# An expert step moved to the last group of attention heads and cut into column-tiled pieces

## Chip, cores and metric

One of the cores of a Trainium2 chip runs the kernel. The metric is the device time of one execution in microseconds (us); lower is better. TensorE (PE) multiplies matrices, VectorE (DVE) and GpSimd (POOL) work elementwise and reduce, ScalarE (ACT) applies functions, SyncE (SP) issues transfers. GpSimd issues transfers too; those of GpSimd share one queue, q0.

## What is computed

The input x has 4 sequences of 2048 tokens of 512 numbers. The output is x, plus attention with 16 heads of 32, plus a layer in which every token goes to one of 8 experts, each of which takes its first 100 tokens:

```python
def reference(x, w_qkv, w_out, b_out, mask_logits, w_gate, w_expert, b_expert):
    xn = layernorm(x)
    # attention
    q, k, v = split(xn @ w_qkv)                  # 16 heads of 32
    q, k = spectral_filter(q), spectral_filter(k)
    attn = softmax(q @ k.T / sqrt(32))
    a = (attn @ v) @ w_out + b_out
    # experts
    probs = softmax(xn @ w_gate)                 # 8 experts
    best, gate = argmax(probs), max(probs)
    place = cumsum(one_hot(best)) - 1            # place in the expert's list
    kept = place < 100                           # the first 100 of each expert
    e = gate * kept * (xn @ w_expert + b_expert) # the other tokens get nothing
    return x + a + e
```

All experts have the same weights w_expert, so the layer is one product of at most 800 gathered rows with a 512 x 512 matrix.

## The kernel before

The heads are taken in 16 groups k of four (4 sequences x 4 groups, `NG = 4`). A group has four blocks n of 512 queries, a block has 16 tiles of 128 keys, and the work on one key tile is called a half (`HB = 16` halves a block, `GH = 64` a group); two halves, an even and an odd one, are a window. Groups, blocks and halves are counted from 0; "half 37 of group 15" lies in its block 2.

In each half TensorE makes the scores of four heads (`scores`, 32-row tiles), ScalarE takes their exponentials from PSUM into an even or an odd tile of 1 MB (two ACTIVATEs of 128x1024), and TensorE multiplies the tile of the half before with the values (`products`, 32-column tiles), which VectorE adds to `num`. Beside that TensorE makes scores of a later block once more, only for the row maxima (`max_matmuls`), and VectorE reduces them (`max_reduce`, `part<-array`); they run 42 places, that is 21 halves, ahead, so the last 21 halves of the last group have none. The maxima enter the scores as a product with ones (`shift`, `array<-negm,ones_b`) at the start of each block.

For the sums over keys, a transfer of GpSimd adds the odd tile into the even one (`pair`, `even<-odd`, an accumulating DMA, issued a window later), and GpSimd adds the even tiles of successive windows (`add_to`, two windows later; without maxima VectorE does it, three windows later). There are three odd and five even tiles. In the next block, `close_steps` folds the last tile into row sums on TensorE (half 5), inverts them on VectorE (halves 6 to 13, 64 columns each), multiplies on GpSimd (`divide`, `ot`, half 14), projects with w_out (four pieces at halves 17 to 20, that is, 1 to 4 of the block after) and adds the result y to the output with an accumulating DMA of 1 MB (`out_dram<-y`, half 21). For block 2 of the last group these places are 7, 8 to 11, 12, 12 to 15 and 15. The last block is closed by `close_last` after the loop, into a copy of the output rows that SyncE has loaded before (`y`, named xs there).

Everything is issued in program order on each compute engine (`InOrder`). The extra steps are hung into an agenda by half with `at(half, step, cost=...)`, where a cost of 1 is a projection piece (16 matmuls of 128 rows x 32 columns x 128 outputs, `columns`, lines 417 to 421). `plan(k)` makes the projections of group k + 1 in group k; `spread` (line 899) places its 48 pieces evenly over the halves, given the costs that are already there. Group 15 has no next group and no projections. Where the cost of a half is not zero, the maxima of the second pair of heads may be reduced in one instruction instead of two (line 1095).

The experts (`expert_steps`, lines 568 to 642, placed by `place_experts`, lines 939 to 955) run so, with `start` = half 0 of group 12:

- half 36 of group 12: `begin` loads w_exp and b_exp, reads the four tables of (token, gate) entries that the routing of the last sequence has filled, merges them and clears `xg`, 7 tiles of 128 rows;
- halves 38 to 50: `fetch` gathers the rows of x by indirect DMA; halves 42 to 54: `measure`; half 58: `scale`;
- half 62 of group 12 to half 14 of group 13, every second half: `expert(i)` normalizes a tile on ScalarE, turns the tile before it (four transposes on TensorE, copied to `xt`, one buffer), and multiplies the one before that (four matmuls of 128 x 128 x 512), adds the bias on VectorE and weighs with the gate on ScalarE;
- from half 26 of group 13, a row tile a block: `gather_row` reads the output rows by indirect DMA on GpSimd (half 26 of the block), `add_row` adds on GpSimd two halves later, `scatter_row` writes them back by indirect DMA two halves after that. The seventh is scattered at the start of group 15.

Gather and scatter read and write the whole output as far as dependences are concerned, so each waits for accumulations of y issued before it, and an accumulation after it waits for the scatter.

Of the kernel before, what the change touches and what calls it, by code (L numbers as in the profile page):

```python
# [12 lines left out]
F32 = mybir.dt.float32  # L13
BF16 = mybir.dt.bfloat16
I32 = mybir.dt.int32
AF = mybir.ActivationFunctionType
ALU = mybir.AluOpType
# [8 lines left out]
P = 128  # L26
# [4 lines left out]
QB = 512  # L31
# [70 lines left out]
def attention_and_top1_experts(ctx: ExitStack, tc: tile.TileContext, a: dict, out: bass.AP):  # L102
# [14 lines left out]
    def bank():  # L117

        return array[:, next(turns), :]
# [445 lines left out]

    taken = {}

    def expert_steps():


        def begin():
            w_exp = chunk("w_exp")
            on.sync.dma_start(out=w_exp, in_=a["L0_ffn_w_expert"].rearrange("(r p) n -> p r n", p=P))
            b_exp = work.tile([P, DM], F32, tag="b_exp", name="b_exp", bufs=1)
            on.sync.dma_start(out=b_exp, in_=a["L0_ffn_b_expert"].partition_broadcast(P))
            entries = small.tile([P, NTAB, ST, 2], F32, name="entries")
            for i, table in enumerate(tables):
                on.sync.dma_start(out=entries[:, i], in_=table.rearrange("(t p) c -> p t c", p=P))
            entry = small.tile([P, ST, 2], F32, name="entry1")
            for i, op in enumerate((ALU.min, ALU.max)):  # L580
                on.vector.tensor_reduce(
                    entry[:, :, i], entries[:, :, :, i].rearrange("p n t -> p t n"), AX.X, op
                )
            who = small.tile([P, ST], I32, name="who")
            on.vector.tensor_copy(who, entry[:, :, 0])
            xg = [chunk("xg"), small.tile([P, ST - TQ, DM], F32, name="xg1")]
            for half in xg:
                on.gpsimd.memset(half, 0.0)
            mv = small.tile([P, ST, 2], F32, name="mv1")
            index = [bass.IndirectOffsetOnAxis(ap=who[:, i : i + 1], axis=0) for i in range(ST)]  # L590
            bound = {"bounds_check": B * S - 1, "oob_is_err": False}
            taken.update(mv=mv, w_exp=w_exp, b_exp=b_exp, entry=entry, index=index, bound=bound, xg=xg)

        def row(i):
            return taken["xg"][i // TQ][:, i % TQ, :]
# [15 lines left out]
            on.gpsimd.tensor_scalar(shift, shift, -1.0, None, ALU.mult)  # L611
            taken.update(rstd=rstd, shift=shift)

        def expert(i):

            if i >= 2:
                at = slice(i - 2, i - 1)
                pe = bank()
                for r in range(NR):
                    on.tensor.matmul(  # L620
                        pe,
                        lhsT=taken["xt"][:, r * P : (r + 1) * P],
                        rhs=taken["w_exp"][:, r, :],
                        start=(r == 0),
                        stop=(r == NR - 1),
                    )
                on.vector.tensor_tensor(row(i - 2), pe, taken["b_exp"], ALU.add)
            if 1 <= i <= ST:
                px = bank()
                for r in range(NR):  # L630
                    on.tensor.transpose(px[:, r * P : (r + 1) * P], row(i - 1)[:, r * P : (r + 1) * P], ident)
                taken["xt"] = work.tile([P, QB], F32, tag="byx", name="xt", bufs=1)
                on.scalar.copy(taken["xt"], px)
            if i >= 2:
                on.scalar.activation(row(i - 2), row(i - 2), AF.Copy, scale=taken["entry"][:, at, 1])
            if i < ST:
                at = slice(i, i + 1)
                on.scalar.activation(
                    row(i), row(i), AF.Identity, bias=taken["shift"][:, at], scale=taken["rstd"][:, at]
                )  # L640

        return begin, fetch, measure, scale, expert

    def gather_row(i):
        taken["sum"] = work.tile([P, DM], F32, tag="byx", name="yg", bufs=1)
        on.gpsimd.indirect_dma_start(taken["sum"], None, out_rows, taken["index"][i], **taken["bound"])

    def add_row(i):
        row = taken["xg"][i // TQ][:, i % TQ, :]
        on.gpsimd.tensor_tensor(row, row, taken["sum"], ALU.add)  # L650

    def scatter_row(i):
        row = taken["xg"][i // TQ][:, i % TQ, :]
# [285 lines left out]
    def place_experts(start):  # L939


        begin, fetch, measure, scale, expert = expert_steps()
        first = start + 36
        at(first, begin)
        for i in range(ST):
            at(first + 2 + 2 * i, fetch, i)
            at(first + 6 + 2 * i, measure, i)
        at(first + 22, scale)
        for i in range(ST + 2):
            at(first + 26 + 2 * i, expert, i, cost=(NR if i >= 2 else 0) + (1 if 1 <= i <= ST else 0))  # L950
        for i in range(ST):
            free = start + GH + i * HB + 26
            for step in (gather_row, add_row, scatter_row):
                at(free, step, i)
                free += 2

    def plan(k):

# [87 lines left out]
    for block in range(1, B * NG * NQ):  # L1046

        costs[block * HB - 5] += 0.25
    place_experts((B - 1) * NG * GH)
    for k in range(B * NG):  # L1050
        plan(k)

# [107 lines left out]
```

## Time and profile before

| | us |
|---|---|
| median of 3 runs | 4195.3 (4194.85 to 4196.63) |
| the profiled execution | 4199.95 |
| its span, first to last instruction | 4197.9 |
| TensorE busy | 4154.1 |
| VectorE busy | 3436.8 |
| GpSimd busy | 2968.2 |
| ScalarE busy | 2493.4 |

In the groups of instructions, the columns are line, engine, operation, written and read tiles, shapes, count, then busy time, mean ns of one, and the idle time before them with what ended it. All have line 82 (the helper that pins the order), so one goes by the tiles' names.

```profile
L82 DVE TENSOR_REDUCE part<-array 128x1 f32<-128x512 f32 (+1 forms) x3129 | 2484.2, 849 | 671.1 <-PE array L82 662.4
L82 POOL TENSOR_TENSOR even<-even 128x1024 f32<-128x1024 f32 x876 | 2121.7, 2524 | 434.6 <-DMA even<-odd 433.6
L82 PE MATMUL array<-keys,q 32*128 32x512 f32 x8192 | 2061.1, 613 | 15.8 <-DVE part L82 5.8
L82 PE MATMUL array<-q,steps_of_keys 32*128 32x512 f32 x8192 | 2029.3, 615 | 2.4 <-ACT odd L82 2.3
L82 ACT ACTIVATE odd<-array 128x1024 f32<-128x1024 f32 x1024 | 995.7, 1021 | 489.4 <-PE array L82 412.7
L82 PE MATMUL array<-xnT,w 128*32 128x128 f32 x16384 | 527.4, 273 | 1.4 <-DVE part L82 0.6
```

An f32 matmul stands in the trace as two records, so 8 records of w_exp are 4 matmuls and 32 of a projection piece are 16. The queue of GpSimd carries most of the traffic; the columns are packets, MB and the share of 16 DMA engines' time:

```profile
q0 software_dynamic: 110432, 605.83, 73.8%
q1 hardware_dynamic: 67952, 71.34, 5.3%
```

### The profile page before, as it was taken

How to read it: one execution, taken by the hardware profiler on the slowest of the kernel's cores; microseconds unless marked ns; L12 is line 12 of the kernel's file. 1: busy time of each engine (PE TensorE's matmuls, PEld its weight loads, DVE VectorE, ACT ScalarE, POOL GpSimd, SP SyncE). 2: the span in 40 equal slices, each digit the busy share in tenths (PEclk: the TensorE clock that was granted, in tenths of full speed). 3: DMA queues.
4: the chain of work that ended last, by engine and by line, in shares of the span. 5: the costliest groups of instructions: out<-in, count | busy, mean ns of one | idle time of the engine just before them, and what ended most of it. 6: DMA issues, size and time to landing. Idle time of an engine off the chain costs nothing.

```text
span 4197.9 us, 121495 instructions
## 1 busy us (share of the span) xinstructions
PE 4154.1 (99%) x52846; PEld 1852.0 (44%) x52846; DVE 3436.8 (82%) x4952; ACT 2493.4 (59%) x3436; POOL 2968.2 (71%) x2052
## 2 busy tenths in 40 slices
PE   8999999999999999999999999999999999999998
PEld 5444444444444444444444444444444443444432
DVE  7778888977888888897788888888778888788896
ACT  4555566675655556657565556666656555556665
POOL 1578676776876777776687766767668776677873
PEclk9999999999999999999999999999999999999999
DMA  3677878987787788898678778799877986778788
GB/s 120 141 149 154 163 152 168 222 194 144 144 166 157 152 160 161 194 202 183 137 155 163 155 156 159 156 200 202 173 151 142 183 162 132 152 159 167 154 168 176
DMA packets 178990, 684.97 MB, mean 163 GB/s; under 512 B 23494, under 2 KB 53352, under 8 KB 113176
## 3 DMA queue, kind: packets, MB, share of 16 engines
q0 software_dynamic: 110432, 605.83, 73.8%
q1 hardware_dynamic: 67952, 71.34, 5.3%
q8 instruction: 414, 6.78, 0.6%
q14 instruction: 120, 0.98, 0.1%
q10 hardware_dynamic: 72, 0.03, 0.0%
HBM read 71.07 MB, written 87.91 MB: 38 GB/s over the span
## 4 chain that ended last, share of the span: by engine, by line
PE 93%; DVE 4%; DMA 1%; issue 1%; ACT 1%; POOL 0%; SPq 0%; ACTq 0%; POOLq 0%; DVEq 0%
PE array L82 93%; DVE part L82 3%; DMA even<-odd 1%; DVE num L82 1%; DVE factor L82 0%; ACT odd L82 0%; POOL even L82 0%; DMA odd<-in_L_attn_w_qkv_dram 0%; DMA w<-in_L_attn_w_qkv_dram 0%; ACT even L82 0%; POOL ot L82 0%; DVE even L82 0%; ACT keys L82 0%; ACT xs L82 0%; SPq L82 0%
## 5 line engine op out<-in xcount | busy, mean ns | idle before, releaser
L82 DVE TENSOR_REDUCE part<-array 128x1 f32<-128x512 f32 (+1 forms) x3129 | 2484.2, 849 | 671.1 <-PE array L82 662.4
L82 POOL TENSOR_TENSOR even<-even 128x1024 f32<-128x1024 f32 x876 | 2121.7, 2524 | 434.6 <-DMA even<-odd 433.6
L82 PE MATMUL array<-keys,q 32*128 32x512 f32 x8192 | 2061.1, 613 | 15.8 <-DVE part L82 5.8
L82 PE MATMUL array<-q,steps_of_keys 32*128 32x512 f32 x8192 | 2029.3, 615 | 2.4 <-ACT odd L82 2.3
L82 ACT ACTIVATE odd<-array 128x1024 f32<-128x1024 f32 x1024 | 995.7, 1021 | 489.4 <-PE array L82 412.7
L82 ACT ACTIVATE even<-array 128x1024 f32<-128x1024 f32 x1024 | 994.4, 1021 | 446.2 <-PE array L82 427.4
L82 PEld LDWEIGHTS array<-keys,q 32*128 32x128 f32 x8192 | 772.1, 184 | 583.5 <-DVE part L82 350.1
L82 PEld LDWEIGHTS array<-q,steps_of_keys 32*128 32x128 f32 x8192 | 691.6, 183 | 259.4 <-issue 228.6
L82 POOL DMA_DIRECT2D even<-odd x510 | 469.7, 922 | 377.7 <-ACT odd L82 318.1
L82 DVE TENSOR_TENSOR num<-num,array 128x512 f32<-128x512 f32 x960 | 650.8, 678 | 17.8 <-PE array L82 17.6
L82 PEld LDWEIGHTS array<-xnT,w 128*32 128x32 f32 x16384 | 458.4, 110 | 257.5 <-DVE part L82 175.9
L82 PE MATMUL array<-even,v 128*32 128x512 f32 x4096 | 545.5, 605 | 0.8 <-DVE part L82 0.8
L82 PE MATMUL array<-odd,v 128*32 128x512 f32 x4096 | 545.9, 605 | 0.0
L82 PE MATMUL array<-xnT,w 128*32 128x128 f32 x16384 | 527.4, 273 | 1.4 <-DVE part L82 0.6
L82 PEld LDWEIGHTS array<-w,xnT 128*32 128x32 f32 x8192 | 229.8, 110 | 148.1 <-DVE part L82 102.8
L82 DVE RECIPROCAL factor<-den 128x64 f32<-128x64 f32 x504 | 274.7, 546 | 0.0
L82 PE MATMUL array<-wo,ot 128*32 128x512 f32 x2048 | 266.9, 594 | 5.0 <-POOL ot L82 5.0
L82 PE MATMUL array<-w,xnT 128*32 128x128 f32 x8192 | 269.7, 273 | 1.8 <-DMA w<-in_L_attn_w_qkv_dram 1.6
L82 PEld LDWEIGHTS array<-even,v 128*32 128x32 f32 x4096 | 80.5, 108 | 389.7 <-DVE part L82 378.6
L82 PEld LDWEIGHTS array<-odd,v 128*32 128x32 f32 x4096 | 80.8, 108 | 388.5 <-DVE part L82 378.4
L82 POOL DMA_DIRECT2D out_dram<-y x63 | 85.9, 1364 | 197.4 <-ACT y L82 125.8
L82 ACT COPY q<-array 128x128 f32<-128x128 f32 x256 | 67.9, 265 | 181.1 <-PE array L82 177.3
(129 smaller groups left out, 1484.5 us busy)
## 6 DMA issues: line engine op xcount, KB each, us to landing
even<-odd POOLq DMA_DIRECT2D x510, 1024.0 KB
out_dram<-y POOLq DMA_DIRECT2D x63, 1024.0 KB
xs<-in_L_attn_x_dram SPq DMA_DIRECT2D x96, 256.0 KB
out_dram<-in_L_attn_x_dram SPq DMA_DIRECT2D x16, 1024.0 KB
w<-wd SPq DMA_DIRECT2D x30, 256.0 KB
w<-in_L_attn_w_qkv_dram SPq DMA_DIRECT2D x16, 256.0 KB
wo<-in_L_attn_w_out_dram SPq DMA_DIRECT2D x16, 256.0 KB
negm<-row SPq DMA_DIRECT2D x192, 4.0 KB
```

What stands on the lines that cost most here:

```text
L82: done = act(*args, **kwargs)
```

## The change

The expert step is placed against group 15, the last one (`place_experts` is called with its first half). `begin` is divided: loads and table reads at half 18 of group 14, merging the tables and clearing xg (`sort`) at half 26, then fetches at halves 28 to 40, measurements at 41 to 53 and `scale` at 58. In group 15 the steps of a row tile i take five of the halves that are not 1 to 5 of a block: `normal` two halves ahead, `turn` (cost 0.5), then four `multiply` (cost 1), each for 128 of the 512 outputs with `columns`, with its own bias add of 128x128 on VectorE, and `weigh`. Turns stand at halves 0, 10, 15, 25, 30, 40 and 45, the pieces between them, the last at half 54. `xt` lies alternately in the weight buffers w0 and w1, which no projection uses any more, and gathered output rows in w2 (w1 for the last) and the old buffer. Rows 0 and 1 are gathered at half 24, added at 27 and scattered at 28; rows 2 and 3 at 40, 43, 44; rows 4, 5 and 6 at 56, 59, 60. The last copy of output rows (y) is loaded after those scatters in program order. The work of the layer is the same.

```diff
+    def spent_weights(s):
+        return weights.tile([P, NR, P], F32, name=f"w{s}", bufs=1).rearrange("p r n -> p (r n)")
+
+    def spare_row():
+        return work.tile([P, DM], F32, tag="byx", name="yg", bufs=1)
...
-        def expert(i):
-
-            if i >= 2:
-                at = slice(i - 2, i - 1)
-                pe = bank()
-                for r in range(NR):
-                    on.tensor.matmul(
-                        pe,
-                        lhsT=taken["xt"][:, r * P : (r + 1) * P],
-                        rhs=taken["w_exp"][:, r, :],
-                        start=(r == 0),
-                        stop=(r == NR - 1),
-                    )
-                on.vector.tensor_tensor(row(i - 2), pe, taken["b_exp"], ALU.add)
...
+        def normal(i):
+            at = slice(i, i + 1)
+            on.scalar.activation(
+                row(i), row(i), AF.Identity, bias=taken["shift"][:, at], scale=taken["rstd"][:, at]
+            )
+
+        def turn(i):
+            px = bank()
+            for r in range(NR):
+                on.tensor.transpose(px[:, r * P : (r + 1) * P], row(i)[:, r * P : (r + 1) * P], ident)
+            taken["xt"] = spent_weights(i % 2)
+            on.scalar.copy(taken["xt"], px)
+
+        def multiply(i, quarter):
+            cols = slice(quarter * P, (quarter + 1) * P)
+            pe = bank()[:, cols]
+            for r in range(NR):
+                columns(
+                    pe,
+                    taken["xt"][:, r * P : (r + 1) * P],
+                    taken["w_exp"][:, r, cols],
+                    start=(r == 0),
+                    stop=(r == NR - 1),
                 )
+            on.vector.tensor_tensor(row(i)[:, cols], pe, taken["b_exp"][:, cols], ALU.add)
+
+        def weigh(i):
+            on.scalar.activation(row(i), row(i), AF.Copy, scale=taken["entry"][:, i : i + 1, 1])
...
     def gather_row(i):
-        taken["sum"] = work.tile([P, DM], F32, tag="byx", name="yg", bufs=1)
-        on.gpsimd.indirect_dma_start(taken["sum"], None, out_rows, taken["index"][i], **taken["bound"])
+        taken["sum", i] = spare_row() if i % 2 else spent_weights(2 if i < ST - 1 else 1)
+        on.gpsimd.indirect_dma_start(taken["sum", i], None, out_rows, taken["index"][i], **taken["bound"])
...
-        first = start + 36
-        at(first, begin)
+        at(start - 46, begin)
+        at(start - 38, sort)
         for i in range(ST):
-            at(first + 2 + 2 * i, fetch, i)
-            at(first + 6 + 2 * i, measure, i)
-        at(first + 22, scale)
-        for i in range(ST + 2):
-            at(first + 26 + 2 * i, expert, i, cost=(NR if i >= 2 else 0) + (1 if 1 <= i <= ST else 0))
+            at(start - 36 + 2 * i, fetch, i)
+            at(start - 23 + 2 * i, measure, i)
+        at(start - 6, scale)
+        halves = iter([start + h for h in range(GH) if not 1 <= h % HB <= TQ + 1])
         for i in range(ST):
-            free = start + GH + i * HB + 26
-            for step in (gather_row, add_row, scatter_row):
-                at(free, step, i)
-                free += 2
+            half = next(halves)
+            at(half - 2, normal, i)
+            at(half, turn, i, cost=0.5)
+            for quarter in range(NR):
+                half = next(halves)
+                at(half, multiply, i, quarter, cost=1)
+            at(half + 1, weigh, i)
+        for block, tiles in ((1, (0, 1)), (2, (2, 3)), (3, (4, 5, 6))):
+            for step, half in ((gather_row, 8), (add_row, 11), (scatter_row, 12)):
+                for i in tiles:
+                    at(start + block * HB + half, step, i)
...
-    place_experts((B - 1) * NG * GH)
+    place_experts((B * NG - 1) * GH)
```

More of the change, by code (lines that the diff above doesn't have):

```diff
@@ L578, in begin, with sort @@
                 on.sync.dma_start(out=entries[:, i], in_=table.rearrange("(t p) c -> p t c", p=P))
+            taken.update(w_exp=w_exp, b_exp=b_exp, entries=entries)
+        def sort():
+            entries = taken["entries"]
             entry = small.tile([P, ST, 2], F32, name="entry1")
@@ L591, in begin @@
             bound = {"bounds_check": B * S - 1, "oob_is_err": False}
-            taken.update(mv=mv, w_exp=w_exp, b_exp=b_exp, entry=entry, index=index, bound=bound, xg=xg)
+            taken.update(mv=mv, entry=entry, index=index, bound=bound, xg=xg)
         def row(i):
@@ L612, in scale @@
             taken.update(rstd=rstd, shift=shift)
-        def expert(i):
-            if i >= 2:
-                at = slice(i - 2, i - 1)
-                pe = bank()
-                for r in range(NR):
-                    on.tensor.matmul(
-                        pe,
-                        lhsT=taken["xt"][:, r * P : (r + 1) * P],
-                        rhs=taken["w_exp"][:, r, :],
-                        start=(r == 0),
-                        stop=(r == NR - 1),
-                    )
-                on.vector.tensor_tensor(row(i - 2), pe, taken["b_exp"], ALU.add)
[L628 to L639, printed above, removed]
-                )
@@ L642, in expert_steps @@
-        return begin, fetch, measure, scale, expert
+        def normal(i):
[9 more added lines that the diff above has]
+            on.scalar.copy(taken["xt"], px)
@@ L644, in gather_row @@
+        def weigh(i):
+            on.scalar.activation(row(i), row(i), AF.Copy, scale=taken["entry"][:, i : i + 1, 1])
+        return begin, sort, fetch, measure, scale, normal, turn, multiply, weigh
     def gather_row(i):
-        taken["sum"] = work.tile([P, DM], F32, tag="byx", name="yg", bufs=1)
-        on.gpsimd.indirect_dma_start(taken["sum"], None, out_rows, taken["index"][i], **taken["bound"])
+        taken["sum", i] = spare_row() if i % 2 else spent_weights(2 if i < ST - 1 else 1)
@@ L648, in add_row @@
+        on.gpsimd.indirect_dma_start(taken["sum", i], None, out_rows, taken["index"][i], **taken["bound"])
     def add_row(i):
         row = taken["xg"][i // TQ][:, i % TQ, :]
-        on.gpsimd.tensor_tensor(row, row, taken["sum"], ALU.add)
+        on.gpsimd.tensor_tensor(row, row, taken["sum", i], ALU.add)
     def scatter_row(i):
@@ L939, in place_experts @@
     def place_experts(start):
-        begin, fetch, measure, scale, expert = expert_steps()
-        first = start + 36
-        at(first, begin)
+        begin, sort, fetch, measure, scale, normal, turn, multiply, weigh = expert_steps()
+        at(start - 46, begin)
+        at(start - 38, sort)
         for i in range(ST):
-            at(first + 2 + 2 * i, fetch, i)
-            at(first + 6 + 2 * i, measure, i)
-        at(first + 22, scale)
-        for i in range(ST + 2):
-            at(first + 26 + 2 * i, expert, i, cost=(NR if i >= 2 else 0) + (1 if 1 <= i <= ST else 0))
-        for i in range(ST):
-            free = start + GH + i * HB + 26
-            for step in (gather_row, add_row, scatter_row):
-                at(free, step, i)
-                free += 2
+            at(start - 36 + 2 * i, fetch, i)
+            at(start - 23 + 2 * i, measure, i)
+        at(start - 6, scale)
+        halves = iter([start + h for h in range(GH) if not 1 <= h % HB <= TQ + 1])
+        for i in range(ST):
+            half = next(halves)
[9 more added lines that the diff above has]
+                    at(start + block * HB + half, step, i)
     def plan(k):
```

## The prediction, before the result

> **What bounds the kernel now.** I read the page's chain first, then the busy time of the last four groups of heads (12 to 15, bounded by the first exponential of each on ScalarE), then block starts on TensorE, then single stretches. In the chain that ended last TensorE has nearly everything:
>
> ```profile
> PE 93%; DVE 4%; DMA 1%; issue 1%; ACT 1%; POOL 0%; SPq 0%; ACTq 0%; POOLq 0%; DVEq 0%
> ```
>
> So work taken off TensorE counts, unless something else ends last in that stage. The windows of groups 12, 13, 14 and 15 (window, its length, then busy time per engine, clock, DMA share and GB/s):
>
> ```profile
> 3176.70:3427.80 251.10, 249.44 (x3261) 109.35 (x3256) 216.48 (x315) 147.80 (x202) 202.07 (x139) 1.00 0.84 169
> 3427.80:3711.80 284.00, 282.93 (x3344) 125.00 (x3340) 216.01 (x316) 159.98 (x221) 194.20 (x129) 1.00 0.72 145
> 3711.80:3961.00 249.20, 248.37 (x3261) 109.95 (x3256) 206.32 (x290) 151.79 (x209) 190.00 (x126) 1.00 0.81 162
> 3961.00:4197.90 236.90, 222.55 (x1650) 72.14 (x1642) 181.08 (x275) 143.41 (x162) 140.41 (x99) 0.99 0.85 170
> ```
>
> Group 13, where the experts run now, is 34 us longer than its neighbours, all of it TensorE busy. Group 15 has no projections for a next group (half as many matmuls) and is still 237 us: other engines and transfers share its bound. That is where the change puts the experts.
>
> **What is removed.** The shift matmuls (negm) mark the start of a block. Groups 9 and 13 stand at the same place of their batch:
>
> ```profile
> 2403.50 0.76 PE L82 MATMUL array<-negm,ones_b 3*128 3x512 bf16 x4
> ...
> 2653.58 0.76 PE L82 MATMUL array<-negm,ones_b 3*128 3x512 bf16 x4
> ...
> 3425.96 0.76 PE L82 MATMUL array<-negm,ones_b 3*128 3x512 bf16 x4
> ...
> 3710.32 0.39 PE L82 MATMUL array<-negm,ones_b 3*128 3x512 bf16 x4
> ```
>
> Group 9 is 2653.58 - 2403.50 = 250.1 us, group 13 is 3710.32 - 3425.96 = 284.4 us. Without experts the projections that `spread` had to cram into its last two blocks lie evenly again, so group 13 becomes a group 9: **-34.3 us**. The least it can be is TensorE's own time in them, 25.9 us of multiplications and 7 x 0.60 us of transposes, 30.1 us. Loading, sorting, seven fetches (1.09 us each on GpSimd), seven measurements (0.66 us on VectorE) and the clearing of xg move from group 12 to 14; group 12 is 250.8 us by its shift matmuls against 249.7 and 249.2 of groups 4 and 8, so some 1.3 us leave there and arrive in group 14: **0** (bounds 0 and +1.3, if group 12 does not get shorter).
>
> **What the pieces cost on TensorE.** A row of the old form, a projection piece, and what follows it:
>
> ```profile
> 3438.57 3.70 PE L82 MATMUL array<-w_exp,xt 128*128 128x512 f32 x8
> ...
> 3928.49 1.06 PE L82 MATMUL array<-xnT,w 128*32 128x128 f32 x32
> 3929.47 0.70 PE L82 MATMUL array<-keys,q 32*128 32x512 f32 x2
> ```
>
> The new quarter (16 matmuls of 128 rows, 32 columns, 128 outputs) has the shape of the projection piece: 3929.47 - 3928.49 = 0.98 us from start to start, 4 x 0.98 = 3.92 us a row against 3.70. TensorE gets no cheaper; what is sought is a place where it has slack. The Trainium skill, page "TensorEngine Tiling (Array Packing)", section "Instruction Overhead", speaks against the form: some 60 cycles for each matmul, and no tiling factor from a dimension that is small already. 448 matmuls take the place of 28; at the 2.4 GHz of the page "TensorE: Matmul & The Clock Gate" (its opening table) that is, as an estimate, 420 x 25 ns = 10.5 us, where the two rows give 7 x 0.22 = 1.5 us; by the page the sum below would be 9 us later. I go by the rows.
>
> How much of a piece shows in group 15 is read from the halves (one key tile each, two exponentials on ScalarE). First exponential of halves 6 and 16 in block 0 of group 14, which has a piece in each of these halves, then of group 15, which has none:
>
> ```profile
> 3735.62 1.94 ACT L82 ACTIVATE even<-array 128x1024 f32<-128x1024 f32 x2 [1.20 <-PE array L82]
> ...
> 3773.66 1.94 ACT L82 ACTIVATE even<-array 128x1024 f32<-128x1024 f32 x2 [1.05 <-PE array L82]
> ...
> 3983.33 1.94 ACT L82 ACTIVATE even<-array 128x1024 f32<-128x1024 f32 x2 [0.60 <-PE array L82]
> ...
> 4017.64 1.94 ACT L82 ACTIVATE even<-array 128x1024 f32<-128x1024 f32 x2 [1.48 <-PE array L82]
> ```
>
> 38.04 against 34.31 us: ten pieces cost 3.73 us, not 9.8, because VectorE (row maxima, sums, reciprocals) holds these halves at 3.4 us anyway. In blocks 0 and 1 two of the ten are turns (transposes, 0.60 us for 0.98), 2 x 0.3 less; half 0 or 16 goes from 3.05 to 3.77 us with a piece, 0.4 with a turn: 3.5 + 3.8 = **+7.3 us**. In block 2, half 32 gives 0.7, halves 38 to 42 18.71 - 16.43 = 2.3 less 0.3 for a turn: **+2.7 us**. The bias add of a quarter is new on VectorE (128x512 takes 0.69 us; 128x128 lies between 0 and that, I take 0.25) and falls into its 0.32 us wait before the next maxima; ScalarE's normalization (0.80), copy (0.59) and weighing (0.72) lie once in five halves in its gap of over 0.6 us: **+0.5 us** for both, bounds 0 and 2.
>
> **What the gathers cost on GpSimd.** Each row block is a gather, an add and a scatter in GpSimd's strict order; now one a block, then two, two and three, all in group 15. One of those of before, and a wait of block 1 in group 15:
>
> ```profile
> 3880.48 1.09 POOL L82 DMA_INDIRECT yg<-out_dram,who  x1 [0.17 <-issue]
> ...
> 3888.45 1.56 POOL L82 TENSOR_TENSOR xg<-xg,yg 128x512 f32<-128x512 f32 x1
> ...
> 3896.95 1.08 POOL L82 DMA_INDIRECT out_dram<-xg,who  x1 [0.18 <-POOL even L82]
> ...
> 4052.65 4.66 POOL L82 TENSOR_TENSOR even<-even 128x1024 f32<-128x1024 f32 x2 [4.36 <-DMA even<-odd]
> ```
>
> 3.7 us a row, 7.5 us for two. The gather reads the output, so it waits for the accumulation issued three halves before; behind it on GpSimd stand the pair transfers (even<-odd), whose landing frees the odd tile that ScalarE writes three windows of two halves later, and the adds, whose end frees even tiles and releases the row sums at half 5 of the next block. GpSimd needs 0.87 + 4.67 us of a window that grows to 7.6 us, so it wins back 2 us a window and has waits of 3.5 and 4.4 us in block 1 to lose first. Placing the instructions on these rows, the lag is made up just about when half 37's row sums need it: **+1.5 us** (bounds 0 and 6, the lag left if nothing is won back before).
>
> **The end.** From half 43 on no maxima are left, halves shrink to 2.5 us, and the chain runs through transfers:
>
> ```profile
> 4126.55 11.07 DMA even<-odd
> ...
> 4146.13 16.15 DMA even<-odd
> ...
> 4167.72 2.02 POOL ot L82
> ```
>
> ```profile
> 4156.00:4161.00 5.00, 5.00 (x36) 1.46 (x32) 1.82 (x4) 2.40 (x3) 0.85 (x1) 1.00 1.05 217
> ```
>
> A pair of 1 MB takes 5 us of the saturated queue, as long as its window. Pieces in halves 43 to 54 (some 5 us) are therefore hidden, and the load of y moves out of the backlog (it will depend on the last scatter; that follows the pair transfer issued at 4169.69, and VectorE takes y up at 4191.10, both shifted alike). Against that: in block 2 two gathers, adds and scatters (7.5 us) delay the last GpSimd adds and pairs, and in block 3 three adds stand ahead of the product ot and wait for gathers queued behind the pairs, 3 to 5 us. By my placing the end comes 8 us later: **+8 us**, bounds 0 (backlog covers all) and 12 (7.5 + 4.5, nothing covered).
>
> **Sum:** -34.3 + 7.3 + 2.7 + 0.5 + 1.5 + 8 = -14.3 us. The profiled execution took 4199.95 us (span 4197.9 and 2.05 around it): 4185.65. The median of the runs is 4.65 us below that execution, 4195.3; so **4181.0 us**, with a range of its own of 4173 to 4189.
>
> **Rivals.** (1) The end hides everything: the +8 falls to 0 and the tiny terms too, 4195.3 - 34.3 + 10 = 4171. For it: the 16 us landing in the chain. Against it: GpSimd stands in that chain just before, at the last adds. (2) GpSimd becomes the bound of blocks 1 to 3: both upper bounds (6 and 12), and ScalarE waits once in each of blocks 1 to 3 for an odd tile, 1.7 us on average (the three such waits of the last block before are 1.4 to 3.0 us), 5 together: 4195.3 - 34.3 + 10 + 23 = 4194, no change. For it: GpSimd is already busy without a gap over stretches of 30 us. Against: it has 96 us idle in group 15 (236.9 - 140.4). (3) **Slower**: a gather that waits on the accumulation's landing holds GpSimd in all three blocks; if that landing takes as long as the longest in the chain (16.15 us) and nothing of it is covered, 3 x 16 = 48 us: 4195.3 - 34.3 + 10 + 48 = 4219. It decides from (34.3 + 8.4 - 10) / 3 = 10.9 us lost a block. For it: the DMA share is over 1.0 just after each accumulation. Against: GpSimd comes to the gather 10 us late anyhow, behind an add that waits for an earlier pair in the same queue. (4) It doesn't do what it says: `spread` leaves group 13 uneven, only 30.1 us are won, 4185; inside the range of the first.
>
> **How the numbers follow.** Forecast with (4) 0.50, rival 1 0.12, rival 2 0.20, rival 3 0.18. A measurement of this kernel tells 0.2% (8.4 us) from no change. Faster by more than that means under 4186.9: nearly all of the forecast, rival 1, little of rival 2: 0.61. Same: rival 2 and the forecast's upper edge, 0.20. Slower 0.19. The range reaches from rival 1 to rival 2: 4170 to 4197.
>
> **What would show it.** Group 13 at 250 us between shift matmuls; w_exp matmuls of 32 columns in group 15 alone, halves 6 to 15 of its block 0 near 38 us; group 15 about 257 us. Rival 2 or 3 shows as ScalarE idle on "DMA even<-odd" or TensorE on "POOL even" in blocks 1 and 2, and gathers with idle time before them that "DMA out_dram<-y" ended. I am wrong if group 13 stays over 255 us, or if group 15's four blocks grow by more than 34 us.

## The result and the profile after

The changed kernel takes 4210.1 us (median of 7 runs, 4206.3 to 4216.0), the kernel before 4195.4 beside it. The ratio is 1.0031, 95% interval 1.0022 to 1.0041: some 13 us slower, where 14 us faster was forecast. The profiled execution took 4212.03 us, its span is 4210.3, 12.4 us longer than before.

The windows of groups 13 and 14, of blocks 0 to 2 of group 15, and of its last block with the tail, each from shift matmul to shift matmul (window, length, busy time of PE, PEld, DVE, ACT and POOL, clock, DMA share, GB/s), after:

```profile
3424.66:3682.74 258.08, 256.20 (x3261) 113.42 (x3259) 210.60 (x315) 148.96 (x201) 179.21 (x117) 1.00 0.78 152
3682.74:3939.54 256.80, 250.41 (x3261) 110.51 (x3258) 214.29 (x307) 152.37 (x210) 191.80 (x130) 0.99 0.82 163
3939.54:4122.34 182.80, 182.05 (x2115) 79.37 (x2113) 148.80 (x231) 116.30 (x140) 135.16 (x92) 1.00 0.78 157
4122.34:4210.30 87.96, 64.45 (x476) 18.44 (x476) 39.77 (x51) 37.17 (x43) 32.21 (x29) 0.87 0.80 174
```

Group 13 lost the experts but not all of their time. Group 14 is 6.4 us longer than its TensorE work. The last block has 23.5 us without TensorE, at a mean clock of 0.87. The same stages of all kernels, each from its own profiled execution:

| kernel | group 13 | group 14 | group 15, blocks 0 to 2 | last block | span | ratio to before, 95% |
|---|---|---|---|---|---|---|
| before | 284.4 | 248.9 | 165.7 | 73.0 | 4197.9 | |
| after | 258.1 | 256.8 | 182.8 | 88.0 | 4210.3 | 1.0031 (1.0022 to 1.0041) |
| a1_order | 250.1 | 256.4 | 183.0 | 86.8 | 4204.1 | 1.0009 (0.9999 to 1.0018) |
| a2_cast | 258.0 | 250.2 | 183.4 | 87.3 | 4207.8 | 1.0011 (1.0001 to 1.0021) |
| a3_norows | 258.0 | 256.4 | 182.0 | 66.2 | 4192.5 | 0.9981 (0.9972 to 0.9991) |
| a4_from_x | 258.1 | 256.2 | 182.9 | 86.9 | 4213.3 | 1.0027 (1.0016 to 1.0038) |
| b1_scatter_add | 258.7 | 256.2 | 182.0 | 85.0 | 4205.3 | 1.0022 (1.0013 to 1.0032) |
| b2_all | 250.1 | 250.2 | 182.0 | 84.7 | 4193.2 | 0.9985 (0.9976 to 0.9995) |
| c1_after_ot | 258.1 | 256.1 | 182.9 | 85.4 | 4205.3 | 1.0024 (1.0015 to 1.0034) |
| d1_whole | 258.0 | 255.8 | 186.0 | 83.2 | 4204.7 | 1.0028 (1.0017 to 1.0038) |
| e1_spread | 250.1 | 250.3 | 182.2 | 72.1 | 4183.5 | 0.9959 (0.9945 to 0.9973) |
| e2_y_early | 250.1 | 250.8 | 182.0 | 85.4 | 4195.9 | 0.9990 (0.9980 to 1.0000) |
| e3_three_steps | 250.1 | 250.8 | 183.2 | 80.9 | 4194.2 | 0.9983 (0.9973 to 0.9992) |
| f1_no_block2_rows | 258.6 | 257.9 | 182.7 | 79.2 | 4208.0 | 1.0006 (0.9994 to 1.0017) |
| f2_no_block3_rows | 258.1 | 257.0 | 183.1 | 82.4 | 4205.4 | 1.0020 (1.0009 to 1.0031) |

Medians aren't set side by side here: the kernel before took between 4195.4 and 4203.4 us on the chips used. The ratios are each to the kernel before on the same chip, and stages are compared inside traces. Group 12, the same work in all kernels but the one before, takes 249.2 us in some of these traces and 250.4 in others, so a stage of one trace is good to about 1 us.

From before to after the stages give -26.3 + 7.9 + 17.1 + 15.0 = +13.7 us; group 12 takes 1.5 us less and what lies ahead of it 0.2 more, and the sum is the 12.4 us of the spans. Three places are dearer than forecast: groups 13 and 14 and the last block. Each is looked up below.

**Group 13.** The timeline of ScalarE in it, after (start, duration, engine, operation, idle time before and its releaser; each pair of exponentials is a half):

```profile
3578.37 2.16 ACT L82 ACTIVATE odd<-array 128x1024 f32<-128x1024 f32 x2 [1.11 <-issue]
...
3588.70 0.27 ACT L82 COPY v<-array 128x128 f32<-128x128 f32 x1 [1.83 <-PE array L82]
3589.84 1.94 ACT L82 ACTIVATE even<-array 128x1024 f32<-128x1024 f32 x2 [0.88 <-PE array L82]
```

Half 39 lasts 11.5 us, from exponential to exponential, since the results of eight projection pieces are copied in it. Halves 31, 35 and 43 are crowded too (6.9, 7.3 and 7.2 us), while the first 31 halves hold only 12 pieces: none lies in halves 16 to 30, and nine of these take 3.05 to 3.5 us, where a half with one piece takes some 3.8. In the code, `CROWDED` (line 44) still names group 14, whose projections group 13 makes. That puts keys early in the list (line 477), and keys can't be placed before half 31 (`SPENT`). The pieces run in the order of the list, so everything behind the keys waits as well.

**Group 14.** The timeline of VectorE, GpSimd and TensorE around half 27, where the tables are merged, after:

```profile
3789.28 5.34 DVE L82 CAST who<-entry 128x7 int32<-128x7 f32 x1
3791.18 3.41 POOL L82 MEMSET xg<- 128x2048 f32 x2
3791.48 3.14 DVE L82 TENSOR_REDUCE part<-array 128x1 f32<-128x512 f32 x3
3794.70 1.94 PE L82 MATMUL array<-even,v 128*32 128x512 f32 x8 [4.59 <-DVE part L82]
```

Before, the same CAST beside the same memset:

```profile
3316.98 3.41 POOL L82 MEMSET xg<- 128x2048 f32 x2
...
3320.21 0.21 DVE L82 CAST who<-entry 128x7 int32<-128x7 f32 x1
```

Seven numbers a partition take 5.34 us instead of 0.21. The CAST starts beside an addition of GpSimd (3788.90 to 3791.53) and ends when the second of the two memsets does (3791.18 + 3.41 = 3794.59). In the kernel before it ended with the memsets as well (3320.42 against 3320.39), but it had come up for its turn only near the end. The maxima behind it start at 3791.48, as the addition ends, and end together with the CAST, at 3794.62; TensorE's products, which wait for them, start at 3794.70.

**The last block.** GpSimd's timeline from the end of block 2 on, after:

```profile
4126.37 1.09 POOL L82 DMA_INDIRECT out_dram<-xg,who  x1 [0.18 <-issue]
4129.48 1.83 POOL L82 DMA_INDIRECT out_dram<-xg,who  x1 [2.03 <-PE array L82]
4131.32 1.29 POOL L82 TENSOR_TENSOR ot<-num,factor 128x512 f32<-128x512 f32 x1
4132.52 2.81 POOL L82 DMA_DIRECT2D even<-odd  x3
...
4162.63 1.10 POOL L82 DMA_INDIRECT w<-out_dram,who  x1 [7.01 <-DMA out_dram<-y]
...
4174.21 1.55 POOL L82 TENSOR_TENSOR xg<-xg,w 128x512 f32<-128x512 f32 x1 [6.82 <-DMA w<-out_dram,who]
...
4179.15 1.26 POOL L82 TENSOR_TENSOR ot<-num,factor 128x512 f32<-128x512 f32 x1
...
4188.83 1.02 POOL L82 DMA_INDIRECT out_dram<-xg,who  x1 [6.20 <-issue]
4192.41 0.98 POOL L82 DMA_INDIRECT out_dram<-xg,who  x1 [2.55 <-DMA out_dram<-xg,who]
```

The first product ot comes 9.0 us into the block (0.5 before), the second 56.8 us into it (42.8 before), and three pair transfers go out together at 4132.52, 10.2 us into the block; before, two of them went at 1.7 and the third at 8.2 us. Behind the gathers stand the adds, behind the adds ot, and behind ot the next pair, all in program order. The scatters at the end stand one behind another: the trace names no releaser for the wait of 6.20 us, but the scatter before it, issued at 4181.56, landed 6.5 us after its issue. What the transfer engines did meanwhile is in the windows of 5 us from the block's start, after:

```profile
4122.34:4127.34 5.00, 3.16 (x54) 1.54 (x54) 0.03 (x1) 1.12 (x2) 4.82 (x3) 1.00 0.91 184
4127.34:4132.34 5.00, 2.99 (x16) 0.71 (x16) 3.16 (x4) 2.76 (x3) 2.97 (x3) 1.00 0.24 92
```

and before:

```profile
4124.89:4129.89 5.00, 4.61 (x34) 1.27 (x30) 0.69 (x1) 2.59 (x3) 3.77 (x4) 1.00 1.01 252
4129.89:4134.89 5.00, 5.00 (x38) 1.42 (x40) 2.96 (x3) 4.22 (x6) 0.88 (x1) 1.00 1.07 239
```

The second number from the right is the DMA share. Before, the queue is full from the start. After, it stands nearly empty in the second window (0.24) while GpSimd is held, in the block that lives on transfers. The whole last block of before:

```profile
4124.89:4197.90 73.01, 60.37 (x416) 15.56 (x412) 39.95 (x49) 36.91 (x43) 15.34 (x17) 0.97 0.85 179
```

Share times length is the time that the transfers took: 0.85 x 73.01 = 62.1 us before, 0.80 x 87.96 = 70.4 after. So of the 15.0 us that the block grew, some 8 are more transfer time and some 7 are idle time of the transfer engines; an idle queue is not the whole of it.

### The profile page after: what moved, and what is told of

Same layout as the page of the kernel before. It is cut to its first block, busy times and chain, and to the rows that moved or that the text cites. A ratio compares the mean times of both kernels' runs of the same rounds, so it can differ in the third digit from the quotient of the medians.

```text
span 4210.3 us, 123158 instructions
## 1 busy us (share of the span) xinstructions
PE 4149.3 (99%) x53686; PEld 1865.0 (44%) x53686; DVE 3438.2 (82%) x4954; ACT 2491.9 (59%) x3436; POOL 2969.6 (71%) x2052
## 5 line engine op out<-in xcount | busy, mean ns | idle before, releaser
L82 PEld LDWEIGHTS array<-q,steps_of_keys 32*128 32x128 f32 x8192 | 692.2, 184 | 257.0 <-issue 228.4
L82 PEld LDWEIGHTS array<-odd,v 128*32 128x32 f32 x4096 | 80.9, 108 | 390.6 <-DVE part L82 380.7
L82 ACT COPY q<-array 128x128 f32<-128x128 f32 x256 | 67.9, 265 | 187.2 <-PE array L82 183.4
```

Of the source, the lines that this page charges most:

```text
L82: done = act(*args, **kwargs)
```

## The experiments

In diffs, only the lines that differ from the changed kernel are shown. "Last block" means block 3 of group 15 with the tail.

### One part undone or left out: a1 to a4

a1_order takes the name of group 14 out of `CROWDED`:

```diff
-CROWDED = (1, (B - 1) * NG + 2)
+CROWDED = (1,)
```

> The changed kernel, but group 14 is no longer in CROWDED, so its projections are placed in group 13 in the ordinary order (values, queries, keys). Theory A (the crowded order, made for a group 13 with experts in it, leaves that group's first 31 halves with 12 pieces and puts 4 to 8 pieces into single halves later): group 13 falls from 258.1 to 250 us, the time by some 8 us, 4202 against 4210. Rival B (group 13 is longer because the gap left by the experts lets GpSimd's pair transfers bunch up): group 13 stays at 256 to 258 us and the time at 4210.

a2_cast has the CAST done by GpSimd, in order with the memset:

```diff
-            on.vector.tensor_copy(who, entry[:, :, 0])
+            on.gpsimd.tensor_copy(who, entry[:, :, 0])
```

> The changed kernel, but the conversion of the token numbers to integers (who, 128x7) runs on GpSimd instead of VectorE. Theory A (the conversion on VectorE, 5.34 us instead of 0.21, cannot run beside GpSimd's add and the clearing of xg that follows it, and holds VectorE, so TensorE waits 4.6 us and its clock falls): the 10.7 us half of group 14 becomes a 4 us half, group 14 falls from 256.8 to about 250 us, the time to 4203. Rival B (VectorE waits there for the table reads, or the clearing of xg alone is what holds it): the long half stays, 4210.

a3_norows leaves out the gathers, adds and scatters, so the experts' results are computed and never added:

```diff
-        for block, tiles in ((1, (0, 1)), (2, (2, 3)), (3, (4, 5, 6))):
-            for step, half in ((gather_row, 8), (add_row, 11), (scatter_row, 12)):
-                for i in tiles:
-                    at(start + block * HB + half, step, i)
+            pass
```

> The changed kernel without any gather, add and scatter of expert rows: the expert part is computed but not added to the output, the rest is the same. Theory A (the rows cost by waits on GpSimd and on transfers, above all in the last block): the last block with its tail goes from 88 us to about 74 us, blocks 0 to 2 of group 15 from 182.8 to about 178 us, the time to 4191. Rival B (the pieces on TensorE and the shorter slack of the queue cost it, not the rows): the last block stays above 83 us, the time above 4204.

a4_from_x gathers rows of x instead of output rows, so that no gather depends on an accumulation:

```diff
-        on.gpsimd.indirect_dma_start(taken["sum", i], None, out_rows, taken["index"][i], **taken["bound"])
+        on.gpsimd.indirect_dma_start(taken["sum", i], None, rows, taken["index"][i], **taken["bound"])
```

> The changed kernel, but the gathers before the adds read rows of the input x instead of the output, so they wait for no accumulation of y; the number and size of all transfers is the same, the expert rows get x added instead of the sum so far. Theory A (the wait for the accumulation's landing, 7.0 us on GpSimd at half 56, then the wait for the gathers behind the pairs, delays ot): the 7.0 us wait is gone, ot comes 6 to 7 us earlier, the time is 4203 to 4205. Rival B (the saturated queue sets the end, it does not matter when the gathers are issued): ot moves by under 2 us, the time stays above 4208.

**a1** brings group 13 to 250.1 us, and nothing else moves by more than 1.2. The same stretch of ScalarE's timeline in a1, one copy between the exponentials of two halves:

```profile
3578.15 1.94 ACT L82 ACTIVATE even<-array 128x1024 f32<-128x1024 f32 x2 [0.60 <-PE array L82]
3580.76 0.27 ACT L82 COPY keys<-array 128x128 f32<-128x128 f32 x1 [0.68 <-PE array L82]
3581.93 1.94 ACT L82 ACTIVATE odd<-array 128x1024 f32<-128x1024 f32 x2 [0.91 <-PE array L82]
```

These halves last 3.8 us each. The stale order cost 8.0 us, all that group 13 was over the forecast.

**a2** brings group 14 to 250.2, 6.6 us less. VectorE's timeline there:

```profile
3793.23 0.23 DVE L82 TENSOR_REDUCE entry<-entries 128x7 f32<-128x28 f32 x2
3793.37 2.42 DVE L82 TENSOR_REDUCE part<-array 128x1 f32<-128x512 f32 x3
```

The maxima follow the merge at once, and the CAST on GpSimd takes 0.46 us. So one CAST in the wrong place cost 6.6 us. TensorE's wait of 4.6 us is the larger part; the rest is TensorE at a lower clock behind the wait, where the products took 1.94 instead of 1.06 us and the projection piece 1.93 instead of 1.06. The Trainium skill, page "SBUF — State Buffer", section "Who interferes with whom", says that a cast on VectorE can take a port pair that it shares with GpSimd, and that the later of the two then stands still until the other's instruction is done. The trace agrees that the CAST ends with a GpSimd instruction, but not with the one that it started beside: an addition and both memsets passed before it ended. That the two share a port is the page's account; no run here shows it apart.

**a3** splits group 15 into pieces and rows. Its windows of blocks 0 to 2 and of the last block:

```profile
3944.34:4126.31 181.97, 181.62 (x2114) 79.07 (x2111) 148.61 (x230) 116.07 (x140) 130.46 (x85) 1.00 0.81 159
4126.31:4192.50 66.19, 57.45 (x480) 16.96 (x476) 40.05 (x51) 37.11 (x44) 12.44 (x14) 1.00 0.87 180
```

Pieces alone make blocks 0 to 2 longer by 16.3 us (182.0 against 165.7), and the last block shorter by 6.8 (66.2 against 73.0): net 9.5 us. The transfers catch up meanwhile: at 180 GB/s the last block moves 11.9 MB, before, at 179 GB/s, 13.1, so about one pair of 1 MB less is left to it. The rows cost 0.8 us in blocks 0 to 2 and 21.8 in the last block, more there than the 14 us that were expected.

**a4** gains next to nothing (86.9 us against 88.0). The gather no longer waits before its issue, and the first add of the three waits longer behind it:

```profile
4159.35 1.10 POOL L82 DMA_INDIRECT w<-in_L_attn_x_dram,who  x1 [0.30 <-issue]
...
4177.52 1.30 POOL L82 TENSOR_TENSOR xg<-xg,w 128x512 f32<-128x512 f32 x1 [12.44 <-DMA w<-in_L_attn_x_dram,who]
```

In after the two waits were 7.01 and 6.82, here it is one of 12.44: the queue of transfers sets when the gathered rows are there, whatever the gather waited for. So a named releaser was not the cause; without it the same work ended no earlier.

### Another order, another form: b1, b2, c1, d1

c1_after_ot moves the three adds and scatters of the last block behind ot:

```diff
-            for step, half in ((gather_row, 8), (add_row, 11), (scatter_row, 12)):
+            for step, half in ((gather_row, 8), (add_row, 12 if block == 3 else 11), (scatter_row, 13 if block == 3 else 12)):
```

> The changed kernel, but in the last block the three adds stand one half later and the scatters too, so that on GpSimd they come behind the product ot instead of ahead of it; transfers are the same. Theory A (the adds, which wait for gathers queued behind pairs, hold ot, which TensorE waits for): ot starts when VectorE's factor is done, some 7 us earlier, and the last block with its tail goes from 87.9 to about 80 us, the ratio to before from 1.0031 to about 1.0012. Rival B (the volume of the gathers in the saturated queue is the price): ot may move, but the pairs behind the gathers end as late, and the last block stays above 85 us. Rival C (the chain of scatters, each waiting for the one before, then y's load, takes over): the last block lies between 82 and 87 us with VectorE waiting for y at the end.

b1_scatter_add drops gather and add; the scatter itself adds (an accumulating indirect transfer), still in bunches:

```diff
-        on.gpsimd.indirect_dma_start(out_rows, taken["index"][i], row, None, **taken["bound"])
+        on.gpsimd.indirect_dma_start(out_rows, taken["index"][i], row, None, compute_op=ALU.add, **taken["bound"])
...
-            for step, half in ((gather_row, 8), (add_row, 11), (scatter_row, 12)):
-                for i in tiles:
-                    at(start + block * HB + half, step, i)
+            for i in tiles:
+                at(start + block * HB + 12, scatter_row, i)
```

> The changed kernel, but gather, add and scatter of a row tile are replaced by one indirect transfer that adds the rows to the output where they lie, at the place of the scatter; the result is the same but for rounding. 7 transfers instead of 14 and no adds on GpSimd. Theory A (waits of the adds for gathers ahead of ot, GpSimd's time in blocks 2 and 3): the last block falls from 87.9 towards the 66 us without rows, 70 to 74 us, the ratio to before to about 0.9993. Rival B (each such transfer waits for the one before it and for the accumulations, and y's load waits for the last): the last block stays above 78 us.

b2_all is a1, a2 and b1 together.

> The changed kernel with the ordinary order of projections in group 13, the integer conversion on GpSimd, and the rows added by one indirect transfer each. If the three parts add up: group 13 at 250 us, group 14 at 250 us, the last block at 70 to 74 us; the ratio to before some 1.0031 - 0.0019 - 0.0016 - 0.0037 = 0.996, faster than both. If a part's gain only uncovers another bound, the ratio stays above 0.998.

d1_whole multiplies with whole columns, 4 matmuls of 128 x 128 x 128 a quarter in place of 16 column tiles:

```diff
-                columns(
+                on.tensor.matmul(
```

> The changed kernel, but each piece of 128 outputs is four matmuls of 128 columns instead of sixteen of 32, at the same places. Theory A (the form is neutral, the two rows of the trace before say 0.98 us a piece of sixteen and 0.93 us a quarter of the old row): blocks 0 and 1 of group 15 stay within 1 us of 62.9 and 61.9 us. Rival B (many small matmuls cost by their number, some 60 cycles each by the Trainium skill's page TensorEngine Tiling (Array Packing), section Instruction Overhead): a block with eight pieces loses some 3 us, 59 to 60 us. Rival C (whole columns cannot overlap with the tiled matmuls beside them): blocks 0 and 1 get longer, over 64 us.

**c1** has ot 6.5 us earlier in its block (50.3 us against 56.8), and the block ends only 2.6 us earlier. GpSimd's timeline:

```profile
4170.23 1.25 POOL L82 TENSOR_TENSOR ot<-num,factor 128x512 f32<-128x512 f32 x1 [5.29 <-DVE factor L82]
...
4183.73 1.02 POOL L82 DMA_INDIRECT out_dram<-xg,who  x1 [5.32 <-issue]
...
4190.20 1.39 POOL L82 DMA_DIRECT2D out_dram<-y  x1 [1.86 <-DMA out_dram<-xg,who]
```

The scatters wait one for another, and the accumulation of y stands behind the last. What was won at ot is lost there: the time from ot to the end grew from 31.2 to 35.1 us.

**b1** was to be clearly shorter if the count of steps were the cost. It takes 85.0 us in the last block. The bunches stay, and each scatter waits for the landing of the one before, in b2:

```profile
4114.23 1.55 POOL L82 DMA_INDIRECT out_dram<-xg,who  x1 [4.03 <-PE array L82]
4115.26 1.82 POOL L82 TENSOR_TENSOR ot<-num,factor 128x512 f32<-128x512 f32 x1
4116.47 3.30 POOL L82 DMA_DIRECT2D even<-odd  x3
...
4168.18 1.55 POOL L82 DMA_INDIRECT out_dram<-xg,who  x1 [6.43 <-DMA out_dram<-xg,who]
```

The first of these waits is put down to a PE array, which a scatter doesn't read; like the others it stands right behind a scatter. Again three pairs go out together. **b2** is then 1.0 - 0.9985 = 0.15% faster than before, with its last block at 84.7 us where 70 to 74 was expected: a1's and a2's gains add up in it (8.6 and 6.0 us against b1, and the ratio falls by 0.0037, some 15 us).

**d1** makes the three blocks 1.0, 1.4 and 0.8 us longer and the last block 4.7 shorter; its ratio, 1.0028, is that of the changed kernel within the intervals. A quarter takes 1.16 us of TensorE in d1 and 1.06 in after. Sixteen small matmuls are a little cheaper here than four large ones, so the form of the pieces is not where the time went. By the page "TensorEngine Tiling (Array Packing)" of the Trainium skill, section "Instruction Overhead", and the 25 ns that the prediction made of its figure, d1 should, as an estimate, have been (448 - 112) x 25 ns = 8.4 us better; its blocks 0 to 2 are 3.2 us worse, and the ratio shows no such gain.

### The rows spread: e1 to e3

All three build on b2 (e3 with the three steps kept instead of the adding scatter). e1_spread places the row tiles singly:

```diff
-        for block, tiles in ((1, (0, 1)), (2, (2, 3)), (3, (4, 5, 6))):
...
+        for i, half in enumerate((12, 16, 28, 32, 44, 48, 60)):
+            at(start + half, scatter_row, i)
```

> The run b2_all with its seven indirect adds no longer two, two and three together but one at a time soon after a row tile is weighed: halves 12, 16, 28, 32, 44, 48 and 60. Theory A (three row transfers in a row, each waiting for the landing of the one before, then y's load and VectorE's wait for y, are what held the last block at 84.6 us): only one stands ahead of y's load, the last block falls to between 66 and 72 us, the ratio to before to about 0.995. Rival B (the indirect adds disturb the pairs in the shared queue wherever they stand): blocks 0 to 2 grow by some 3 to 6 us, the last block stays above 75 us, the ratio at or above 0.997.

e2_y_early loads the last copy of output rows one window earlier, ahead of the last three scatters, so rows of the last 512 tokens can lack what those add:

```diff
-                if last and w == NW - 2:
+                if last and w == NW - 3:
```

> The run b2_all, but the last copy of output rows (y) is loaded two halves earlier, ahead of the last three row adds, so that rows which these add to the last 512 tokens, if there are any, would be missing. Theory A (the wait for y, 3.3 us on VectorE, and what is behind it): the last block falls by 3 to 5 us, to 80 or 82 us, no more, since the closing stores still wait for the chain of row adds and the accumulation of y. Rival B (the load of y is the whole difference to the 66 us without rows): it falls to 66 to 70 us. Rival C (something earlier in the last block holds it): it stays at 84 us.

e3_three_steps keeps gather, add and scatter at the places of e1:

```diff
+        for i, half in enumerate((12, 16, 28, 32, 44, 48, 60)):
+            for step, later in ((gather_row, -3), (add_row, 0), (scatter_row, 1)):
+                at(start + half + later, step, i)
```

> The run e1_spread with the three steps of the changed kernel instead of the indirect add: a tile's gather three halves ahead, its add at the half given there, its scatter one later; with the ordinary order of projections and the integer conversion on GpSimd. Theory A (the bunching of the rows was the fault, not their form): the last block stays within 4 us of that of e1_spread, the ratio below 0.997. Rival B (adds that wait on GpSimd for gathers are a cost of their own): the last block is over 6 us longer than in e1_spread and GpSimd waits over 5 us for a gather's landing there.

**e1** has the last block at 72.1 us, 12.6 less than b2 with the same seven scatters. GpSimd's timeline:

```profile
4108.80 1.88 POOL L82 TENSOR_TENSOR ot<-num,factor 128x512 f32<-128x512 f32 x1
...
4152.08 2.04 POOL L82 TENSOR_TENSOR ot<-num,factor 128x512 f32<-128x512 f32 x1 [9.27 <-DVE factor L82]
...
4155.24 1.61 POOL L82 DMA_INDIRECT out_dram<-xg,who  x1 [0.30 <-issue]
```

No scatter waits for another for longer than 0.64 us, the first ot starts 2.6 us before the block begins (at 4111.41), and the second waits for VectorE, as it did before the change. The windows from the block's start show the queue full again:

```profile
4111.41:4116.41 5.00, 5.00 (x68) 2.22 (x68) 3.54 (x5) 2.61 (x4) 3.35 (x3) 1.00 1.03 204
4116.41:4121.41 5.00, 5.00 (x46) 1.53 (x40) 3.05 (x3) 4.81 (x7) 0.90 (x1) 1.00 1.10 211
```

This kernel takes 4185.3 us (5 runs, 4182.3 to 4186.7) against 4201.3 of the kernel before on that chip, ratio 0.9959 (0.9945 to 0.9973): it beats both.

**e2** leaves the last block at 85.4 us: when y is loaded makes no difference. **e3** takes 80.9, so spread out the three steps still cost 8.8 us more in that block than one adding scatter. No add waits for a gather there, as the rival had it; but the first ot comes 8.2 us into the block, behind an add, a scatter and a gather that waits 2.0 us for that scatter. Both things count, the bunches and what stands on GpSimd ahead of ot.

### Which rows: f1 and f2

f1 leaves out the adding of rows 2 and 3, f2 that of rows 4 to 6:

```diff
-        for block, tiles in ((1, (0, 1)), (2, (2, 3)), (3, (4, 5, 6))):
+        for block, tiles in ((1, (0, 1)), (3, (4, 5, 6))):
```

> The changed kernel without gather, add and scatter of rows 2 and 3 (those of block 2); rows 0, 1, 4, 5 and 6 stay. Theory A (in block 2 the rows hold GpSimd back by some 8 us just before the last block, so ot and the pairs start late and the transfer engines, busy 0.24 and 0.72 of the first two stretches of 5 us there, stand idle; the rows of block 3 cost another 14 us by the adds ahead of ot and the chain of scatters): the last block with its tail falls from 87.9 to 78 to 81 us and its first 10 us have a transfer share of about 1.0. Rival B (the rows of block 3 cost everything): 86 us or more. Rival C (rows of block 2 cost everything, since all of block 3 is the same queue shifted): 66 to 70 us.

```diff
-        for block, tiles in ((1, (0, 1)), (2, (2, 3)), (3, (4, 5, 6))):
+        for block, tiles in ((1, (0, 1)), (2, (2, 3))):
```

> The changed kernel without gather, add and scatter of rows 4, 5 and 6 (those of the last block); rows 0 to 3 stay. Theory A: the last block falls from 87.9 to 72 to 76 us, with the transfer share of its first 10 us still at about half. Rival B: 66 to 69 us. Rival C: 84 us or more.

f1 saves 8.8 us of the last block, f2 5.5. f1 fell where it was expected, but the transfer share of its first 10 us, expected at about 1.0, is 0.55 in the first window of 5 us and 1.04 in the second; f2, at 82.4 us, missed its 72 to 76. In f1 the first ot comes 0.2 us into the block, as before the change, and the adds still hold the second one. In f2 it is the other way about:

```profile
4131.44 1.33 POOL L82 TENSOR_TENSOR ot<-num,factor 128x512 f32<-128x512 f32 x1
4132.72 2.77 POOL L82 DMA_DIRECT2D even<-odd  x3
...
4174.56 2.04 POOL L82 TENSOR_TENSOR ot<-num,factor 128x512 f32<-128x512 f32 x1 [10.42 <-DVE factor L82]
```

GpSimd is in time for the second ot and waits for VectorE, but its first ot came 8.5 us into the block and that was never won back. Taken alone, the rows of block 2 are the dearer part. Together the two save 14.3 of the 21.8 us that a3 saves. The remaining 7.5 us go only when both are gone; how they divide, no run here tells.

## Why the prediction was wrong

In the terms of the prediction's own sum, measured as differences of stages:

| term | forecast | measured | off by |
|---|---|---|---|
| group 13 without experts | -34.3 | -26.3 | +8.0 |
| begin to measure moved from group 12 to 14 | 0 | -1.5 + 7.9 = +6.4 | +6.4 |
| pieces in group 15 (TensorE, VectorE, ScalarE), with what the end hides | 7.3 + 2.7 + 0.5 = 10.5 | 16.3 - 6.8 = 9.5 | -1.0 |
| rows on GpSimd, in the blocks and at the end | 1.5 + 8 = 9.5 | 0.8 + 21.8 = 22.6 | +13.1 |
| sum | -14.3 | +12.2 | +26.5 |

(Ahead of group 12 are the 0.2 us left to the 12.4.) Of the two signs by which the prediction wanted to be found wrong, the first came: group 13 stayed over 255 us. The second did not: group 15 grew by 32.0 us, under 34.

**What bounds the kernel: right.** TensorE in groups 13 and 14, VectorE in the halves without pieces, transfers in the last block.

**"The projections that `spread` had to cram into its last two blocks lie evenly again, so group 13 becomes a group 9": failed, 8.0 us.** The cramming was taken for a consequence of the experts' costs. It is that of an order of projections chosen for a group with experts, and the order stays when the experts go. a1 shows it: with the plain order group 13 is the 250.1 us that was forecast. Rival 4 left group 13 uneven, but by 4.2 us only.

**"Some 1.3 us leave there and arrive in group 14: 0": failed, 6.4 us.** The instructions were counted, their durations taken from the trace, and each is right but one. The CAST of 0.21 us had its duration only because it started near the end of the memset. Moved, it stood beside an addition and both memsets, and took 5.34 us; without it on VectorE 6.6 us go (a2).

**What the pieces cost: the number right, by luck.** Two errors cancel. Without the rows (a3) blocks 0 and 1 are 11.3 us longer than before, where the sum has 7.3, and block 2 is 5.0 longer, where it has 2.7. Ten pieces were to take 3.7 us more in a block than none. The ten halves 6 to 15 of block 0 take 39.3 us, 5.0 more than before, and with those from half 43 on the three blocks are 16.3 us longer. But the end hid 6.8 us of it, more than the pieces from half 43 on (a3). Rival 1 named this cover; without the rows it would have had the better account of the end.

**What the gathers cost, and the end's "+8 us, bounds 0 and 12": failed, 13.1 us.** The instructions were laid out one after another on GpSimd with the waits of one gather, add and scatter of before. Each had been alone in its block there. In a bunch they are not seven times one. The wait for gathers in the last block was put at 3 to 5 us; it is 7.0 us before they are issued and 6.8 behind them, and a4 shows that the queue sets it (12.4 us). The wait of a scatter for the landing of the scatter before it (2.0 us behind the rows of block 2, 6.2 and 2.55 in the last block) is not in the sum at all. The first ot of the last block, with three pairs behind it, and the second stand behind all of that in program order. The 7.5 us for the rows of block 2 were in the upper bound and fit what f1 saves (8.8); but the sum let the backlog of transfers cover a part, and f1 shows no cover: while GpSimd was late, the queue ran nearly empty (0.24). The bound of 12 was the sum of busy times and short waits, so it was no bound. The placing "just about when half 37's row sums need it" was right: blocks 0 to 2 lost 0.8 us to the rows, though in block 1 a scatter waited 2.7 us behind another as well.

**The rivals.** None gives the result. Rival 3 alone has the sign, and its 4219 is nearest, but its mechanism falls: without any wait for an accumulation's landing (a4) the last block stays, and block 1 lost nothing. Rival 2's GpSimd does become the bound, in the last block alone.

## What to carry to other kernels

When a step is moved away, look for the schedule that was written to live with it, an order, a table of exceptions, a cost, and take it away too. Dependent transfers that were cheap one at a time are not cheap in bunches: place them singly, and never ahead of the instruction on the same engine that feeds the queue which bounds the stage. A duration in the trace holds for its neighbours of that moment; a tiny instruction that shares something with a long one on another engine has to be priced by the long one.

## What the runs showed of the hardware

- A CAST of 128x7 on VectorE lasted 5.34 us beside an addition and two memsets of GpSimd, while a reduction from PSUM beside such additions keeps its 2.42 us (3793.37 in a2, where GpSimd adds from 3790.72 to 3795.70).
- TensorE's granted clock falls within one wait. In after, where TensorE waits 4.6 us in group 14, it is 0.77 and then 0.55 in the two windows of 5 us from 3789.5 on, and the product behind the wait takes 1.94 us for 1.06; in the last block it is 0.50 just before ot. Read more finely in the same trace, it stays at 1.00 for the first 2.1 us of that wait, then falls to 0.50, and is back at 1.00 only at 3799.2, 4.5 us after the wait's end. So a wait on TensorE can cost more than its length: 6.6 us (a2) for the 4.6 here, 0.9 of it in a single product.
- The accumulating scatter of 128 rows takes 1.5 to 2.4 us on GpSimd, against 1.0 to 1.8 for the plain one, and saves the gather and an addition of 1.25 to 2.3 us: in e1 against e3 that is worth 8.8 us of the last block.
